# A state space layer: its two outputs summed in PSUM, and one step of its power table made a copy

## The chip, the cores and the metric

The kernel runs on one core of a Trainium2 chip. The metric is the device time of one launch in microseconds (us). A profiled execution of the same program gives, for every engine, when each instruction ran and what it waited for. The engines are TensorE (PE in the profile; its weight loads are PEld), VectorE (DVE), ScalarE (ACT), GpSimd (POOL) and SyncE (SP, which here only issues DMAs). Each engine works through its own queue in order.

## The reference

`x` is (1, 4096, 512). A cross attention layer with a state space part (`_L0_xattn_ref`) is added to it, and then a quantized feed-forward layer with a depthwise convolution (`_L0_ffn_ref`). The part that matters here is the state space layer `s4d`, which convolves each of the 512 channels with a kernel of its own, over all 4096 positions:

```python
def s4d(x, log_dt, A_re, A_im, C_re, C_im, D_skip):
    dt = jnp.exp(log_dt)
    A = A_re + 1j * A_im
    C = C_re + 1j * C_im
    dtA = dt[:, None] * A
    dC = C * (jnp.exp(dtA) - 1.0) / A
    powers = jnp.exp(dtA[:, :, None] * jnp.arange(L))
    K = 2.0 * jnp.einsum('dn,dnl->dl', dC, powers).real
    ...
    y = jnp.fft.irfft(xf * Kf.T[None], n=n, axis=1)[:, :L]   # y = causal convolution of x with K
    return y + x * D_skip
```

A channel has 64 complex states. `powers` holds the powers of exp(dt A) of each state.

## The kernel before

The program has three stages, one after the other: attention (until about 1675 us of the profile), `state_space` (about 1685 to 2222 us) and `feed_forwards` (the rest). The change touches `state_space` alone.

`state_space` cuts the 4096 positions into 32 chunks of 128, and the 512 channels into 8 groups of 64. A channel pair with its 2 x 64 states fills the 128 partitions, so a group is 32 pairs. For a group `g` the work is:

- `powers(g, k)` and `top(g, k)`, for each half `k` of the group (16 pairs): a tile `pt` of 128 x 16 x 2 (real, imaginary) x 128 that holds the powers 0 to 127 of each state. Column 0 is set to 1 + 0i once, by two memsets on POOL for each of the five tiles (L1093, L1094). Each level of a doubling multiplies the columns known so far by the power 2^lv and writes as many new ones: two multiplications into temporaries (L1130, L1131) and a sum into `pt` (L1132), all on DVE, 32 elements per partition at level 0, 64 at level 1, up to 1024 at level 5. The last level, `top`, shares its work between ACT (L1138, 16 instructions) and DVE (L1148, and the sum L1154 in `top_sum`).
- `turn` and `chunk`: transposes of `pt` on PE (L1168), copied out by ACT (L1171), and products with `x` on PE (L1180), copied by ACT (L1184) into `ht`, the state that each chunk adds.
- `scan_inside`, `scan_over`, `scan_into`: DVE turns these into the state at the start of each chunk (`times`, L1200 to L1202, with the sums L1214, L1219 and L1225).
- `outputs`: DVE multiplies the states with the output table (L1235 to L1237, in two halves of 16 chunks; L1239 puts the kernel's own row in front), and ACT copies the products `z` into `sz` (L1242).
- `between(g, u)`, u = 0 to 3: PE multiplies `sz` with `pt` into PSUM (L1255); ACT copies that into a tile `y` (`yg`) of 128 x 4 x 128 (L1261); POOL adds `D_skip` to column 0 (L1263). Partitions 32m of `y` hold the convolution's kernel (128 taps) of a channel; the others hold what earlier chunks give to this one. Eight DMAs for two tiles write the kernel rows to DRAM (`kd`).
- `load_k` reads `kd` back as a Toeplitz matrix `hk`, and `inside(g, u)` multiplies it with `x` on PE: 16 products of 32 rows x 128 columns into one PSUM tile `ps_h` (L1285), which has two buffers.
- `store(g, u)`: one DVE instruction (L1292) reads `ps_h`, adds `y` times `later`, and writes `y`; a DMA writes it to `yT`. `later` is a column of ones with zeros at partitions 0, 32, 64 and 96, so that the kernel rows are not added.

The order is written out by hand: the stage runs under a manual schedule for all five engines, so each engine has its instructions in program order. `round_(g)` for g from -2 to 8 mixes three groups: the scan and the outputs of `g`, the transposes and chunk products of `g + 1`, the powers of `g + 2`, and `inside` and `store` of `g - 1`. In a round, `store(g - 1, 0)` stands ahead of `scan_into(g)`, `store(g - 1, 1)` ahead of `outputs(g)`, and `store(g - 1, 2)` and `store(g - 1, 3)` behind `outputs(g)` and ahead of `turn(g + 1, 6)` and `powers(g + 2, 0)`. `inside(g - 1, u)` stands ahead of `turn(g + 1, u + 3)` and `chunk(g + 1, u + 2)`. Rounds 1 to 5 hold all of this. Rounds -2 to 0 have no `inside` and `store`, rounds 6 to 8 no `powers`, round 7 no `turn` and `chunk`, and round 8 only `inside` and `store` of the last group.

The temporaries of DVE (`temp`) come from one pool of five buffers of 128 x 1024, which are taken again as they come free. In `outputs`, ACT is the last reader of two of them (the two `z`).

Of the kernel before, what the change touches and what calls it, by code (L numbers as in the profile page):

```python
# [10 lines left out]
F32 = mybir.dt.float32  # L11
# [4 lines left out]
ALU = mybir.AluOpType  # L16
# [4 lines left out]
P = 128  # L21
# [853 lines left out]
LEVELS = 7  # L875
# [178 lines left out]
def state_space(env, io, tabs, x1r, yT):  # L1054
# [8 lines left out]
    tc, nc, ident = env.tc, env.nc, env.ident  # L1063
    with ExitStack() as ctx:
        def pool(name, bufs, **kw):
            return ctx.enter_context(tc.tile_pool(name=name, bufs=bufs, reuse_waits="tile", **kw))
# [11 lines left out]
        one = pool("s_one", 1)  # L1078
# [8 lines left out]
        tab, ptab, pts, tops, xg, ht, zs, bts, yg, hk, phs = ({} for _ in range(11))  # L1087
# [8 lines left out]
        def temp(n):  # L1096
            t = tmp.tile([P, 1024], F32, name="tmp")
            return t[:, :n]
# [18 lines left out]
        def powers(g, k):  # L1117
            q = slice(k * NSB, (k + 1) * NSB)
            pt = pts[g, k] = power_tiles[(2 * g + k) % len(power_tiles)]
            for lv in range(LEVELS - 1):  # L1120
                n = 2**lv
                sh = [P, NSB, 2, n]
                t1, t2 = (
                    temp(NSB * 2 * n).rearrange("p (q r n) -> p q r n", q=NSB, r=2)
                    for _ in range(2)
                )
                old = pt[:, :, :, :n]
                wr = ptab[g][:, 3 * lv, q].unsqueeze(2).unsqueeze(3).to_broadcast(sh)
                wi = ptab[g][:, 3 * lv + 1 : 3 * lv + 3, q].rearrange("p s q -> p q s")
                mul(t1, old, wr)  # L1130
                mul(t2, old, wi.unsqueeze(3).to_broadcast(sh))  # L1131
                add(pt[:, :, :, n : 2 * n], t1, t2[:, :, ::-1, :])  # L1132
# [147 lines left out]

        def inside(g, u):
            py = phs[g, u] = ps_h.tile([P, 4, P], F32, name="ps_h")
            for c in range(16):
                r = slice(32 * (c % 4), 32 * (c % 4) + 32)
                nc.tensor.matmul(  # L1285
                    py[r, c // 4, :], xg[g][:, :, 16 * u + c], hk[g, u, c // 8][:, c % 8, :],
                    start=True, stop=True,
                )

        def store(g, u):  # L1290
            y = yg.pop((g, u))
            nc.vector.scalar_tensor_tensor(y, y, later, phs.pop((g, u)), ALU.mult, ALU.add)  # L1292
            c0 = g * GC + 16 * u
            nc.sync.dma_start(
                bass.AP(yT.tensor, yT.offset + c0 * T, [[P, P], [4 * T, 4], [1, P]]), y
            )


        later = one.tile([P, 1], F32, name="later")
        dskip = one.tile([P, NPAIR // 2], F32, name="dskip")  # L1300
        sz = one.tile([P, 2, 2, NT, GP], F32, name="sz")
        load(0, 0, T_CHUNK)
        load(0, T_CHUNK, NTAB)
        nc.sync.dma_start(dskip, io["D_skip"])
        nc.gpsimd.memset(later, 1.0)
        for m in range(4):
            nc.gpsimd.memset(later[32 * m : 32 * m + 1, :], 0.0)

        def zeros():
            nc.gpsimd.memset(sz[:64, :, 1, :, :], 0.0)  # L1310
# [7 lines left out]
        def round_(g):  # L1318
# [16 lines left out]
            for u in range(4):  # L1335
                if back:
                    inside(g - 1, u)
                    if u < 2:
                        load_k(g - 1, u + 2)
                if n1 and u < 3:  # L1340
                    turn(g + 1, u + 3)
                    chunk(g + 1, u + 2)
                if back and u < 2:
                    store(g - 1, u)
                if u == 0 and now:
                    scan_into(g)
# [6 lines left out]
            if back:  # L1353
                store(g - 1, 2)
                store(g - 1, 3)
# [3 lines left out]
            if n2:  # L1359
                powers(g + 2, 0)  # L1360
                top(g + 2, 0)
# [14 lines left out]
            if n2:  # L1376
                powers(g + 2, 1)
                top_sum(g + 2, 0)
                top(g + 2, 1)
# [565 lines left out]
def block_kernel(tc, io, out):  # L1945
    with ExitStack() as ctx:
        env = Env(tc, ctx)
        env.n_tiles = NT
        dp = ctx.enter_context(tc.tile_pool(name="scratch", bufs=1, space=DRAM))
        x1r = dp.tile([T, D], F32, name="x1r")  # L1950
        film_out = dp.tile([T, 2 * D], F32, name="film_out")
        tabs = dp.tile([NTAB, P, NPAIR], F32, name="tabs")
        yT = dp.tile([D, T], F32, name="yT")
        x2 = dp.tile([T, D], F32, name="x2")
        xq = dp.tile([D, T], BF16, name="xq")
        dq = dp.tile([T], F32, name="dq")
        undo = env.c.tile([P, 2], F32, name="undo")

        def rest():
            state_space(env, io, tabs, x1r, yT)  # L1960
            feed_forwards(env, io, film_out, yT, x2, xq, dq, undo, out)

        bad = env.c.tile([P, 1], I32, name="bad")
        with tc.tile_pool(name="flags", bufs=1, reuse_waits="tile") as fp:
            missed = fp.tile([P, NT * H], F32, name="missed")
            masked = fp.tile([P, 1], F32, name="masked")
            env.nc.gpsimd.memset(masked, 0.0)
            attention(env, io, x1r, film_out, missed, masked, tabs)
            unlike(env, missed, masked, bad)
        rest()  # L1970
        n = env.nc.values_load(bad[0:1, 0:1], min_val=0, max_val=P * NT * H + G)
        with tc.If(n > 0):
            attention_general(env, io, x1r, film_out)
            rest()
# [71 lines left out]
```

## Time and profile before

| | |
|---|---|
| timed runs (us) | 3597.01, 3689.06, 3704.32; median 3689.06 |
| the profiled execution: its time | 3598.88 us |
| its span | 3597.1 us |
| busy in the span: PE, PEld, DVE, ACT, POOL | 3100.3, 1894.4, 3047.9, 1995.1, 976.4 us |
| granted TensorE clock over the span | 0.907 of full speed |
| `store` L1292, DVE, 128x512 | 32 instructions, mean 749 ns |
| copy of `y` L1261, ACT, 128x512 from PSUM | 32 instructions, mean 589 ns |
| levels 0 of `powers`, DVE, 128x32: L1130, L1131, L1132 | 16 of each, mean 200, 198 and 215 ns |

A row of the timeline has the start, the time that it lasts, the engine, the line, what is written from what, and a count where like instructions are merged; in brackets stands the idle time before it and what ended it. A matmul on float32 operands leaves two records, so `inside` with its 16 products shows x32. Consecutive DVE instructions overlap a little, so the time from one start to the next says better what an instruction costs than its own duration.

### The profile page before, as it was taken

The page shows a single profiled execution, that of the slowest core. Times are in us where ns is not written, and L with a number is a line of the kernel's source. Part 1 is how long each engine was busy: PE and PEld are TensorE (multiplying, and loading weights), DVE is VectorE, ACT ScalarE, POOL GpSimd, SP SyncE. Part 2 cuts the span into 40 slices and gives each one's busy share as a digit, 9 for nine tenths or more (in the row PEclk, how much of TensorE's full clock was granted, in tenths as well). Part 3 has the DMA queues.
Part 4 walks back from the last instruction along what each step waited for, and adds up shares of the span by engine and source line. Part 5 has one row for each costly group of instructions (what it writes and reads, how often), then busy time and mean ns, then how long its engine had stood idle before and what let it go on. Part 6 is the DMA issues. An engine that isn't in the chain of part 4 may idle for free. (4 is left out here: it accounts for less than half of the span.)

```text
span 3597.1 us, 48276 instructions
## 1 busy us (share of the span) xinstructions
PE 3100.3 (86%) x14970; PEld 1894.4 (53%) x15014; DVE 3047.9 (85%) x9455; ACT 1995.1 (55%) x3739; POOL 976.4 (27%) x1623
## 2 busy tenths in 40 slices
PE   7899999999999999994777774989998999999975
PEld 3444444444444444442776773656665666666642
DVE  5999999999999999988899984777777777777777
ACT  3777777777777777762655541124444444444445
POOL 2222232223333332221000001223433333334422
PEclk8899999999999999997777775999999999999987
DMA  7676766677666667664254437732223333232211
GB/s 197 128 135 136 142 132 132 134 144 140 136 136 136 131 131 145 132 134 118 47 126 103 125 80 239 216 95 55 55 63 57 63 62 68 55 69 55 52 33 47
DMA packets 355862, 394.19 MB, mean 110 GB/s; under 512 B 112741, under 2 KB 249959, under 8 KB 355210
## 3 DMA queue, kind: packets, MB, share of 16 engines
q0 software_dynamic: 51872, 161.82, 25.2%
q1 hardware_dynamic: 303722, 229.20, 25.0%
q8 instruction: 120, 1.97, 0.2%
q14 instruction: 148, 1.21, 0.1%
HBM read 171.31 MB, written 62.15 MB: 65 GB/s over the span
## 5 line engine op out<-in xcount | busy, mean ns | idle before, releaser
L597 DVE MAX8 cand<-s 128x8 f32<-128x89 f32 (+1 forms) x4608 | 715.3, 243 | 18.1 <-ACT s L584 18.1
L693 PE MATMUL po<-ctxn,aT 124*128 124x384 f32 (+1 forms) x1664 | 642.2, 531 | 14.4 <-ACT aT L681 14.3
L1533 PE MATMUL ph<-hT,w 128*128 128x256 f32 x2048 | 498.9, 388 | 0.5 <-ACT hT L1522 0.5
L1544 PE MATMUL po<-w,gt 128*128 128x512 f32 x1024 | 481.6, 592 | 0.0
L1690 ACT ACTIVATE cv<-pb,cb,cw 128x256 f32<-128x256 f32 (+1 forms) x272 | 149.8, 551 | 597.2 <-DVE pb L1687 591.3
L584 ACT ACTIVATE s<-ps 128x802 f32<-128x802 f32 (+1 forms) x512 | 400.2, 835 | 133.7 <-PE ps L580 133.6
L693 PEld LDWEIGHTS po<-ctxn,aT 124*128 124x128 f32 (+1 forms) x1664 | 327.5, 207 | 278.5 <-issue 75.6
L655 ACT ACTIVATE s<-s,lb 128x1601 f32<-128x1601 f32 x256 | 419.2, 1638 | 98.6 <-POOL lb L644 98.4
L619 DVE SCALAR_TENSOR_TENSOR s<-s,m 128x3202 f32<-128x3202 f32 x128 | 455.4, 3558 | 6.8
L1533 PEld LDWEIGHTS ph<-hT,w 128*128 128x128 f32 x2048 | 384.0, 195 | 61.2 <-issue 10.0
L718 PE MATMUL po<-wvf,acT 128*128 128x512 f32 x768 | 363.8, 610 | 0.6 <-ACT acT L708 0.6
L1699 DVE SCALAR_TENSOR_TENSOR cv<-pb,cw,cv 128x256 f32<-128x256 f32 (+1 forms) x544 | 252.6, 464 | 46.6 <-ACT cv L1690 36.9
L1678 PE MATMUL pb<-xw,w1q 128*128 128x258 bf16 (+1 forms) x1088 | 172.9, 285 | 123.5 <-DVE cv L1699 113.5
L659 POOL DMA_DIRECT2D s<-s x96 | 129.4, 1348 | 545.8 <-ACT s L655 180.4
L1768 POOL TENSOR_TENSOR cv<-cv,scb 128x512 f32<-128x512 f32 (+1 forms) x136 | 181.0, 1347 | 323.5 <-ACT scb L1763 323.5
L580 PE MATMUL ps<-kT,qT 32*128 32x401 f32 (+1 forms) x2048 | 259.9, 552 | 8.3 <-ACT s L584 8.3
L1687 DVE TENSOR_TENSOR pb<-pb,sx 128x258 f32<-128x258 f32 (+1 forms) x272 | 112.1, 412 | 182.1 <-PE pb L1678 180.5
L1544 PEld LDWEIGHTS po<-w,gt 128*128 128x128 f32 x1024 | 192.3, 190 | 134.3 <-issue 118.6
L1678 PEld LDWEIGHTS <-w1q 128*128 128x128 bf16 x1088 | 102.8, 103 | 290.9 <-DVE cv L1699 174.2
L718 PEld LDWEIGHTS po<-wvf,acT 128*128 128x128 f32 x768 | 135.3, 189 | 181.0 <-issue 164.0
L676 PE MATMUL pt<-ident,s 128*124 128x128 f32 x832 | 136.2, 293 | 105.3 <-DMA s<-s 84.9
L1538 ACT ACTIVATE gt<-ph,b 128x256 f32<-128x256 f32 x256 | 120.7, 472 | 184.3 <-PE ph L1533 184.1
(310 smaller groups left out, 5017.4 us busy)
## 6 DMA issues: line engine op xcount, KB each, us to landing
s<-s POOLq DMA_DIRECT2D x96, 1602.0 KB, 11.8
hk<-kd SPq DMA_DIRECT2D x64, 512.0 KB
film_out<-f SPq DMA_DIRECT2D x32, 512.0 KB
xt<-in_x SPq DMA_DIRECT2D x63, 256.0 KB
ft<-film_out SPq DMA_DIRECT2D x31, 512.0 KB
qT<-qd SPq DMA_DIRECT2D x128, 64.0 KB
xu<-in_x SPq DMA_DIRECT2D x32, 256.0 KB
x1r<-xr SPq DMA_DIRECT2D x32, 256.0 KB
```

Of the source, the lines that this page charges most:

```text
L580: nc.tensor.matmul(ps[:, j - j0, :n], qT[i][r, h, :], kT[r, h, c0 : c0 + n], start=True, stop=True,)
L584: nc.scalar.activation(sq[:, j0 : j0 + 2, c0 : c0 + n], ps[:, :, :n], AF.Copy, scale=QSCALE * TINY)
L597: nc.vector.max(out=cand[:, :, b], in_=s[:, b * CHW : min((b + 1) * CHW, G)])
L619: nc.vector.scalar_tensor_tensor(s[:, :G], s[:, :G], m8[:, KTOP - 1 : KTOP], s[:, :G], ALU.is_lt, ALU.subtract, accum_out=missed[:, k : k ...
L655: nc.scalar.activation(part, part, AF.Exp, bias=lbs[k][:, 1:2], scale=-1.0 / TINY)
L693: nc.tensor.matmul(pas[i][:, :DV], aTs[i][:w, c, :], ctxn[:w, c, :], start=(c == 0), stop=(c == NG - 1),)
L718: nc.tensor.matmul(po, acTs[i][:, c, :], wvf[:, c, q * D : (q + 1) * D], start=False, stop=(c == NDV - 1),)
L1533: nc.tensor.matmul(ph[:, :W], w1[:, d, c * P : (c + 1) * P], hTs[b][:, d, :], start=(d == 0), stop=(d == ND - 1),)
L1544: nc.tensor.matmul(pos[b * TB + k], gs[b, c][:, k * P : (k + 1) * P], w2[:, c, :], start=(c == 0), stop=(c == NH - 1),)
L1678: nc.tensor.matmul(ph[:, : n + 2], w1q[:, d, c * P : (c + 1) * P], bit["xw", j][:, d, : n + 2], start=(d == 0), stop=(d == ND - 1),)
L1699: nc.vector.scalar_tensor_tensor(cv, ph[:, tap : tap + n], cw[:, c, tap : tap + 1], cv, ALU.mult, ALU.add)
L1768: nc.gpsimd.tensor_mul(cv, cv, bit["scb", j][:, :n].unsqueeze(1).to_broadcast([P, 2, n]))
```

## The change

In `powers`, level 0 is taken out of the loop. Column 0 is 1 + 0i, so column 1 is the first power itself, and one DVE copy writes it from the table:

```diff
-            for lv in range(LEVELS - 1):
+            w = ptab[g][:, 0:2, q].rearrange("p s q -> p q s")
+            nc.vector.tensor_copy(pt[:, :, :, 1], w)
+            for lv in range(1, LEVELS - 1):
```

`later` becomes a 128 x 128 identity whose columns 0, 32, 64 and 96 are zero. In `inside`, PE first multiplies the whole tile `y` by it into `ps_h` (128 x 512, float32), and the 16 products add to that. In `store`, ACT copies the sum from PSUM to `y`:

```diff
         def inside(g, u):
             py = phs[g, u] = ps_h.tile([P, 4, P], F32, name="ps_h")
+            nc.tensor.matmul(
+                py.rearrange("p q l -> p (q l)"), later, yg[g, u].rearrange("p q l -> p (q l)"),
+                start=True, stop=False,
+            )
             for c in range(16):
                 r = slice(32 * (c % 4), 32 * (c % 4) + 32)
                 nc.tensor.matmul(
                     py[r, c // 4, :], xg[g][:, :, 16 * u + c], hk[g, u, c // 8][:, c % 8, :],
-                    start=True, stop=True,
+                    start=False, stop=(c >= 12),
                 )
 
         def store(g, u):
             y = yg.pop((g, u))
-            nc.vector.scalar_tensor_tensor(y, y, later, phs.pop((g, u)), ALU.mult, ALU.add)
+            nc.scalar.copy(y, phs.pop((g, u)))
...
-        later = one.tile([P, 1], F32, name="later")
+        later = one.tile([P, P], F32, name="later")
...
-        nc.gpsimd.memset(later, 1.0)
-        for m in range(4):
-            nc.gpsimd.memset(later[32 * m : 32 * m + 1, :], 0.0)
+        nc.gpsimd.tensor_copy(later, ident)
+        nc.gpsimd.memset(later.rearrange("p (m a) -> p m a", m=4)[:, :, 0], 0.0)
```

## The prediction

> **What bounds the kernel now.** I read the page's slices first, then the busy times of one stretch, then the groups by shape, then the timelines of DVE, ACT and PE over one round. The change lies in slices 19 to 25 (about 1685 to 2222 us), where DVE is fuller than PE and the TensorE clock is low:
>
> ```profile
> PE   7899999999999999994777774989998999999975
> DVE  5999999999999999988899984777777777777777
> PEclk8899999999999999997777775999999999999987
> 1860.00:1920.00 60.00, 45.92 (x448) 43.79 (x448) 57.78 (x104) 30.70 (x87) 2.32 (x5) 0.74 0.48 116
> ```
>
> The last line is one round (round 2 runs from 1860.30 to 1920.54, 60.24 us): PE 45.92 us busy, DVE 57.78, ACT 30.70, clock 0.74. DVE's row has no idle time with a releaser anywhere in it, so what is taken off DVE shortens the round until another engine is late. The groups and DVE's timeline give the prices:
>
> ```profile
> L1292 DVE SCALAR_TENSOR_TENSOR yg<-yg,later,ps_h 128x512 f32<-128x512 f32 x32 | 23.4, 749 | 34.6 <-PE ps_h L1285 34.3
> L1261 ACT COPY yg<-ps_y 128x512 f32<-128x512 f32 x32 | 18.2, 589 | 34.0 <-PE ps_y L1255 18.3 <-issue 14.2 <-DMA kd<-yg 1.4
> L1239 DVE COPY tmp<-tabb 128x64 f32<-128x64 f32 x8 | 1.6, 195 | 0.3
> ...
> 1876.44 0.75 DVE L1292 SCALAR_TENSOR_TENSOR yg<-yg,later,ps_h 128x512 f32<-128x512 f32 x1
> 1877.10 0.62 DVE L1200 TENSOR_TENSOR tmp<-ht,tabb 128x448 f32<-128x448 f32 x1
> ...
> 1895.49 0.20 DVE L1130 TENSOR_TENSOR tmp<-pt,taba 128x32 f32<-128x32 f32 x1
> ...
> 1896.15 0.23 DVE L1130 TENSOR_TENSOR tmp<-pt,taba 128x64 f32<-128x64 f32 x1
> ```
>
> From start to start a `store` costs DVE 0.66 us, and level 0 also 0.66. What can be late next is the chain over ACT and PE in the same round:
>
> ```profile
> 1887.69 0.84 ACT L1184 COPY ht<-ps_u 64x124 f32<-64x124 f32 x4 [1.07 <-PE ps_u L1180]
> 1890.76 2.10 ACT L1242 COPY sz<-tmp 64x1024 f32<-64x1024 f32 x2 [2.23 <-DVE tmp L1239]
> 1894.29 2.10 ACT L1242 COPY sz<-tmp 64x1024 f32<-64x1024 f32 x2 [1.42 <-DVE tmp L1237]
> ...
> 1874.20 2.01 PE L1285 MATMUL ps_h<-hk,xg 128*32 128x128 f32 x32
> 1879.56 1.29 PE L1285 MATMUL ps_h<-hk,xg 128*32 128x128 f32 x32
> 1896.44 6.33 PE L1255 MATMUL ps_y<-pt,sz 128*64 128x128 f32 x64 [4.79 <-ACT sz L1242]
> ...
> 2149.33 0.69 DVE L1200 TENSOR_TENSOR tmp<-ht,tabb 128x512 f32<-128x512 f32 x1 [11.09 <-ACT ht L1184]
> 2165.05 0.75 DVE L1292 SCALAR_TENSOR_TENSOR yg<-yg,later,ps_h 128x512 f32<-128x512 f32 x1 [2.08 <-PE ps_h L1285]
> ...
> 2302.54 1.73 PE po L1544 x4
> ```
>
> ACT waits only 1 to 2 us ahead of its `sz` copies, and PE's first `inside` of the round took 2.01 us where the later ones took 1.29. The last line, from the chain, is two 128x512 float32 products of the feed-forward stage (four records).
>
> **The change part by part.**
>
> *Level 0.* Three instructions (0.66 us) become one copy. The nearest row is L1239, 0.195 us; followed by an instruction that needs its result it takes 0.24 us, as L1132 at level 0 does (1907.40 to 1907.64). Gain 0.42 us a call. Of the 16 calls two (round -1) end in waits for ACT (3.92, 1.11 and 1.72 us before 1744.14) and gain nothing; 14 gain 5.9 us.
>
> *The store on DVE.* 20 instructions lie in rounds 1 to 5: 20 x 0.66 = 13.2 us. In round 6 two stand ahead of `outputs` (1.3 us), and the other two lie ahead of the 11.09 us wait and gain nothing. In round 7 two stand ahead of `outputs`, and the first waits 2.08 us for PE: 3.4 us, all of it ahead of the `sz` copies that PE waits for. The last store of round 8 becomes an ACT copy of 0.59 us (L1261, same shape, also from PSUM): nothing. Sum with level 0: 23.8 us.
>
> *The store on ACT.* Four copies of 0.54 to 0.59 us a round, 2.3 us. ACT is busy 30.7 of 60, and before `sz` it only fills waits. The pair behind `outputs` stands ahead of `turn(6)`'s copies: in rounds 1 to 5 PE is then in `between` (6.33 us), which hides it. In round 6 `turn` 6 and 7 and the chunks follow at once, and DVE waits for them (11.09 us): 1.1 us lost. SP's `yT` DMAs of that pair go out about 2 us later; behind them SP has the table and `x` loads of later groups, and `kd` writes that are not ready for another 10 us.
>
> *The product on PE.* Two records of 512 columns: warm 1.73 / 2 = 0.87 us. Cold, by `inside` (2.01 against 1.29) it is 1.35 us, by L1180 (3.52 against 1.96 in the same round) 1.55; I take L1180's ratio, as it has full-height weights too, and twice the warm price (1.73) as the far end. With 1.55 for the first of a round and 0.87 for three this is 4.2 us a round. `y` is ready a round earlier, so its data costs no wait. Behind it on PE stand `inside`, `turn`, `chunk`; for these waits ACT, whose `ht` copies of chunk 4 stand ahead of `sz`. Three products lie ahead of them (3.3 us): they end at 28.2 + 3.3 = 31.5 us of the round instead of 28.2. DVE will have the first `z` at 30.2 - 1.3 = 28.9. So ACT, not DVE, sets `sz`: its four copies (4.2 us) end at 35.7, against 36.1 today.
>
> *The wait that this adds.* ACT's `sz` copies are the last readers of two of DVE's five temporaries. `powers` comes to the second at its second to fourth level; today that is just after ACT is done (1896.39). With the stores and level 0 gone DVE gets there at about 34.3 us of the round and waits until 35.7, about 1.4 us. At the end of the round the chain through `top`, `between` and chunk 7 now ends 1.2 us ahead of DVE (1919.25 to 1920.54); it shortens with `powers` and stays 0.7 ahead. Bounds: no wait, if the buffers come free in another order; 2.6 us, which is all that the stores gain. I take 1.4 for rounds 1 to 5 (7 us) and 0.5 for round 0, which has no products: 7.5 us.
>
> *The ends.* Round 6: the products delay ACT's `sz` the same way, so its 1.3 us are lost too. Round 7: `inside` waits for `hk`; the products lie in these waits, except some 0.4 us. Round 8: the last two tiles are ready 0.7 to 1.4 us apart, and cold products stand between: 0.6 us lost (0 if warm, 1.0 at 1.73). `later`: POOL's memsets took 0.70 us from 1679.37; a copy of 128x128 lies between 0.18 (L75, one column) and 1.26 us (L1495, four times as wide), nearest perhaps 0.4, plus a memset of 0.12: nothing, within 0.7 either way.
>
> *The sum.* 23.8 - 7.5 - 1.1 - 1.3 - 0.4 - 0.6 = 12.9 us, 0.4%: about 3586 us on the profiled execution's 3598.88 (span 3597.1 and 1.8 around it). That execution lies at the lowest of the three timed runs; the median is 3689.06, 90 us above it, and nothing in this trace says where those 90 us go. I take the difference off the median: 3676 us. The low group, by the same sum 3584, may be the median next time and has to be in the range.
>
> [...] The low price of the product rests on the rows of L1544, where each record has a weight load of its own (190 ns) and still four records take 1.73 us, so the loads are hidden. [...]
>
> **The rivals.** (a) DVE stays the bound everywhere, with no wait at the temporaries: 23.8 less the 1.1 and 0.4 of rounds 6 and 7 is 22 us, 3577 on the profile, 3667 on the median. For it: five buffers, and PE idle 14 of 60 us. Against it: ACT's 1 to 2 us of slack. (b) The products slow DVE. DVE's 128x448 operations take 1.39 and 1.21 us instead of 0.62 at 1879.49 and 1883.19, when `inside` runs, and not when L1255 does. If the products do the same for 4.2 us a round, DVE loses about 2.2 us x 6 rounds = 13: no change, 3600 or 3690. (c) Slower: the chain over PE becomes the round. Every product at 1.73 us puts `sz` at 37.6 and the end of chunk 7 at 59.4 us of the round; DVE, held at the temporaries, ends at 60.2, where it ends now. So above 1.75 us a product the rounds get longer, by four times the excess: at 2.1 us 7 us in rounds 1 to 5, 4 in round 6 and 1.5 in round 8, less the 4 kept outside: 3608 or 3698. Over 2% (72 us) it would need more than 4 us a product, which no row supports. (d) The change does nothing for the end because the round is bound elsewhere already: against it stands DVE's row without a wait.
>
> **How the numbers follow.** My forecast (a gain of 6 to 18 us) has 0.5, (a) 0.2, (b) 0.15, (c) 0.1, (d) 0.05. All of these lie within 2%, which is about what a measurement of this kernel can tell from no change; the three runs themselves lie 3% apart. For that, and for what I have not seen, I leave 0.08 for faster and 0.05 for slower. The likeliest case alone gives 3671 to 3683 on the median. The range goes from the low group with a full gain (3575) to the highest run with no gain (3704), less a little: 3574 to 3700.
>
> **What would show it.** In the changed profile DVE should have no L1292, and its groups of 128x32 should be one copy near 0.2 us. ACT should have 32 copies of 0.59 us at the store. The product should take 0.87 us in most places. A wait of 1 to 2 us on ACT `sz` should stand at one of the first levels of `powers` once a round; rounds should last 58 to 59 us, against 60.24, and 57 without that wait. The forecast is wrong if DVE waits for `ht` at the start of a round, if DVE's rows are longer beside the product, or if the stage from 1685 to 2222 us is longer than now.

## The result, and the profile after

The changed kernel took 3573.26 us, the median of 7 runs (3569.68 to 3682.59), beside 3597.66 us for the kernel before, the median of 7 runs (3594.59 to 3704.32). The ratio is 0.9928, with a 95% interval of 0.9914 to 0.9943: 26 us or 0.7% less, which counts as no change at 2%. Runs of both kernels fall into two groups about 2.8% apart; the ratios compare the lower group alone, two of the three runs that the prediction started from lay in the upper one, and the state space stage is as long in a profile of the upper group (516.8 us) as in one of the lower (516.1).

The profile read here is that of a second run of the changed kernel (label after_again, span 3565.7 us against 3597.1 before). Its slices 19 to 25, round 2 (57.03 us; the columns are those of the line shown before), and groups of the state space stage by shape:

```profile
PE   7899999999999999995687876989989999999975
DVE  5999999999999999998999983777777777777776
PEclk8899999999999999997788787999999999999987
1848.85:1905.88 57.03, 44.55 (x456) 40.12 (x456) 54.87 (x97) 34.20 (x91) 2.87 (x5) 0.85 0.50 122
```

```profile
L1291 PE MATMUL ps_h<-hk,xg 128*32 128x128 f32 x1024 | 47.0, 322 | 16.4 <-DMA hk<-kd 16.4
L1285 PE MATMUL ps_h<-yg,later 128*128 128x512 f32 x64 | 40.9, 726 | 0.0
L1291 PEld LDWEIGHTS ps_h<-hk,xg 128*32 128x32 f32 x1024 | 36.9, 198 | 48.2 <-DMA hk<-kd 24.8 <-issue 23.4
L1298 ACT COPY yg<-ps_h 128x512 f32<-128x512 f32 x32 | 24.9, 801 | 33.6 <-PE ps_h L1291 24.3 <-DMA hk<-kd 8.9
L1203 DVE TENSOR_TENSOR tmp<-ht,tabb 128x448 f32<-128x448 f32 x32 | 24.7, 773 | 0.0
L1121 DVE COPY pt<-taba 128x32 f32<-128x32 f32 x15 | 2.9, 193 | 0.0
```

L1292 is gone from DVE, level 0 is one copy of 193 ns (L1121), and the store is an ACT copy (L1298), of 801 ns in the mean and not the 589 of L1261. DVE is busy 54.87 of 57.03 us where it was busy 57.78 of 60.00, so it is still the fullest engine. PE has the products in addition (L1285, two records each). In round 2 it is yet busy no longer, 44.55 us against 45.92, with the granted clock at 0.85 and not 0.74; over rounds 1 to 5 it is busy 46.2 us a round in the mean against 44.2, and the clock is 0.82 against 0.78.

Cut at the same instructions (the last one that makes the tables, L1050; level 1 of group 0; the start of each round on DVE; the first load of the next stage), the stage fell from 541.92 to 516.09 us:

| Part | before (us) | after (us) | gain | predicted gain |
|---|---|---|---|---|
| tables to level 1 of group 0 | 6.14 | 5.29 | 0.85 | 0.84 for both rows |
| from there to round 0 | 58.38 | 55.38 | 3.00 | |
| round 0 | 55.42 | 54.59 | 0.83 | 0.34 |
| rounds 1 to 5, the mean of one | 60.62 | 57.25 | 3.37 | 2.1 |
| round 6 | 46.65 | 46.22 | 0.43 | -1.1 |
| rounds 7 and 8, to the next stage's load | 72.21 | 68.34 | 3.87 | 2.4 |
| sum (rounds 1 to 5 count five times) | 541.92 | 516.09 | 25.8 | 12.9 |

The other 5.6 us of the span's 31.4 lie in attention and in the feed-forward stage, which the change does not touch. What there is to explain is a gain twice the predicted one, 6.5 us of it in rounds 1 to 5, where the wait that I had put at 1.4 us a round does not show.

### The profile page after: what moved, and what is told of

It reads as the page before. It is cut to its first block, busy times and chain, and to the rows that moved or that the text cites. A ratio compares the mean times of both kernels' runs of the same rounds, so it can differ in the third digit from the quotient of the medians.

```text
span 3668.6 us, 48302 instructions
## 1 busy us (share of the span) xinstructions
PE 3175.3 (87%) x15034; PEld 1918.4 (52%) x15078; DVE 3028.2 (83%) x9391; ACT 2017.1 (55%) x3771; POOL 1197.9 (33%) x1620
## 3 DMA queue, kind: packets, MB, share of 16 engines
q8 instruction: 120, 1.97, 0.2%
## 4 chain that ended last, share of the span: by engine, by line
PE 40%; DVE 31%; ACT 10%; POOL 7%; DMA 6%; issue 5%; SPq 0%; POOLq 0%; ACTq 0%; DVEq 0%
PE po L693 10%; PE ph L1538 8%; PE po L1549 7%; DVE cand L597 4%; DMA s<-s 4%; ACT s L584 3%; PE pp L1789 3%; PE ps L580 2%; DVE s L619 2%; PE pb L1683 2%; PE po L718 2%; ACT s L655 2%; DVE cv L1704 2%; DVE bn_st L69 2%; DVE cv L1722 2%
## 5 line engine op out<-in xcount | busy, mean ns | idle before, releaser
L693 PE MATMUL po<-ctxn,aT 124*128 124x384 f32 (+1 forms) x1664 | 653.7, 539 | 63.7 <-ACT aT L681 63.7
L580 PE MATMUL ps<-kT,qT 32*128 32x401 f32 (+1 forms) x2048 | 289.8, 582 | 79.8 <-ACT s L584 79.8
L580 PEld LDWEIGHTS ps<-kT,qT 32*128 32x128 f32 x2048 | 98.6, 192 | 201.5 <-ACT s L584 122.0
```

Of the source, the lines that this page charges most:

```text
L580: nc.tensor.matmul(ps[:, j - j0, :n], qT[i][r, h, :], kT[r, h, c0 : c0 + n], start=True, stop=True,)
L693: nc.tensor.matmul(pas[i][:, :DV], aTs[i][:w, c, :], ctxn[:w, c, :], start=(c == 0), stop=(c == NG - 1),)
```

## The experiments

The theory after the result: DVE stays the bound in every round, because it comes back to the buffer of the second `z` later than I had put it, after ACT has already let it go. The rivals: the product costs time that something else gives back; the wait is there in another shape; the gain belongs to the copy of level 0 and not to the store. "Stage" below is the table's sum, 541.92 before and 516.09 in the changed kernel.

**The changed kernel again** (after_again, no edit).

> The changed kernel once more, for a profile beside the others. Theory A (DVE is the bound of rounds 0 to 5, the product on PE and the copy on ACT are hidden, and no wait at the temporaries takes anything back): ratio 0.993, about 25 us off, with rounds of 57 us and under 0.5 us of waits for ACT at the levels of the powers. Rival B (the wait at the temporaries and the delay by the products take 8 us back, and something outside the rounds gives it instead): the same time, but rounds 1 to 5 longer than 58 us.

Measured: 0.9943 [0.9929, 0.9957] of the time before; the stage as in the table.

**One part at a time.** copy_alone has only the copy at level 0, psum_alone only the sum in PSUM:

```diff
# copy_alone, against the kernel before
-            for lv in range(LEVELS - 1):
+            w = ptab[g][:, 0:2, q].rearrange("p s q -> p q s")
+            nc.vector.tensor_copy(pt[:, :, :, 1], w)
+            for lv in range(1, LEVELS - 1):
# psum_alone, against the changed kernel
-            w = ptab[g][:, 0:2, q].rearrange("p s q -> p q s")
-            nc.vector.tensor_copy(pt[:, :, :, 1], w)
-            for lv in range(1, LEVELS - 1):
+            for lv in range(LEVELS - 1):
```

> Only the first doubling is a copy; the outputs are added on DVE as before. Theory A: 0.42 us for 14 calls and up to 1 us at the start of the stage, 6 to 8 us off (ratio 0.998). If the whole change gains more than its two parts, or less, they meet somewhere: rival B has the wait at the temporaries only with both, so the parts alone would gain more than the whole.

> Only the product on PE and the copy on ACT; level 0 stays three DVE instructions. Theory A: 20 stores of 0.66 us in rounds 1 to 5, 3.4 us in round 7, nothing in rounds 6 and 8: 16 to 18 us off (ratio 0.995). Rival B: 7 us are lost in waits at the temporaries or behind the products, 9 to 11 us off (0.997).

Measured: copy_alone 0.9978 [0.9968, 0.9988], 7.9 us less, and its stage is 8.1 us shorter; psum_alone 0.9961 [0.9947, 0.9974], 14.0 us less, its stage 17.4 us shorter. The stages add up, 8.1 + 17.4 = 25.5 against 25.8 for both, so neither part lives off the other. Of the copy's 8.1 us, 3.0 lie between level 1 and round 0 (55.34 us, as in the changed kernel; psum_alone has 58.49, where the kernel before has 58.38); rounds 0 to 5 gain what was costed, 0.8 us each in the mean, and rounds 6 to 8 lose 0.8 together.

**Without the product** (no_product: the product is left out, so `y` lacks what earlier chunks give).

```diff
-            nc.tensor.matmul(
-                py.rearrange("p q l -> p (q l)"), later, yg[g, u].rearrange("p q l -> p (q l)"),
-                start=True, stop=False,
-            )
...
-                    start=False, stop=(c >= 12),
+                    start=True, stop=True,
```

> The changed kernel without the product on PE: what earlier chunks give to the output is left out. Theory A: the product is hidden in rounds 1 to 5 and costs at most 1 to 3 us in rounds 6 and 8: within 3 us of the changed kernel. Rival B: the products delay ACT's sz copies and DVE behind them by 1 us a round and more: 6 to 10 us faster than the changed kernel.

Measured: 0.9940 [0.9921, 0.9959]; rounds 1 to 5 last 57.06 us in the mean, against 57.25 with the product, and the stage 516.8 us. The product costs nothing where it stands.

**Two and four products.** Each product starts the PSUM tile anew, so the sum holds `y` once.

```diff
-            nc.tensor.matmul(
+            for rep in range(2):    # four_products: range(4)
+                nc.tensor.matmul(
```

> The changed kernel with the product on PE issued twice for each tile (the second overwrites the first, so the result is the same): about 1 us more of PE per tile, 4 us a round. Theory A: PE and ACT have some 3 us of room before PE's wait for sz becomes DVE's: rounds 1 to 5 grow by 0 to 1 us each, rounds 6 and 8 by 3 to 5 us together; 3 to 10 us slower than the changed kernel. Rival B: the products are on the path already, 3 to 4 us a round, 20 to 25 us slower.

> The product issued four times for each tile (the last counts): about 3 us more of PE per tile, 12 us a round, of which 9 lie ahead of the sz copies. Theory A: past the room of some 3 us each round grows by what is left, 5 to 7 us; with rounds 6 to 8 about 40 to 50 us slower than the changed kernel. Rival B: 9 to 12 us a round from the start, 60 to 70 us slower.

Measured: two_products 0.9953 [0.9939, 0.9967], stage 525.7 us, 9.6 more than with one; by the ratios it is only 3.6 us slower than after_again, and their intervals overlap. The four runs of four_products took 3603.89, 3608.16, 3703.51 and 3710.26 us; its stage takes 556.3 us, and rounds 1 to 5 last 63.26 us, 6.0 more than with one product. DVE now waits for ACT's `sz` copies early in `powers`, though not for the buffer that I had named. DVE's timeline in the kernels with two and with four products, one wait of each, and beside the first ACT's four `sz` copies:

```profile
1941.04 0.29 DVE L1132 TENSOR_TENSOR tmp<-pt,taba 128x128 f32<-128x128 f32 x1 [1.01 <-ACT sz L1244]
```

```profile
1938.41 4.73 ACT L1244 COPY sz<-tmp 64x1024 f32<-64x1024 f32 x4
```

```profile
1959.34 0.43 DVE L1133 TENSOR_TENSOR tmp<-pt,taba 128x256 f32<-128x256 f32 x1 [6.66 <-ACT sz L1244]
```

ACT copies the two `z` one after the other, with two copies for each. The wait until 1941.04 ends as the second of the four copies does, so it is for the first `z`; ACT is through with the second only 2.1 us later. In each of rounds 1 to 5 the waits of both kernels end in this way. So the chain through PE and ACT has room for the first product (about 4 us a round); the second costs 1.1 us a round and the third and fourth 4.9 together. Rival (c) of the prediction had the right place: PE's chain does become the round, but only once there is more than one product.

**The wait, forced.** The changed kernel has five temporaries. four_temps has four; z_at_level_1 keeps five and makes level 1 write into the last `z` itself.

```diff
# four_temps
-        tmp = pool("s_tmp", 5)
+        tmp = pool("s_tmp", 4)
# z_at_level_1
+                if lv == 1 and k == 0 and last_z:
+                    t1 = last_z[0][:, : NSB * 2 * n].rearrange("p (q r n) -> p q r n", q=NSB, r=2)
...
-                z, t = (
-                    temp(NT * GP).rearrange("p (a r q) -> p a r q", r=2, q=GP) for _ in range(2)
-                )
+                zf, tf = temp(NT * GP), temp(NT * GP)
+                last_z[:] = [zf]
+                z, t = (f.rearrange("p (a r q) -> p a r q", r=2, q=GP) for f in (zf, tf))
```

> The changed kernel with four temporaries of DVE instead of five, so that the powers come to a buffer that ACT still reads at level 2 and not at level 5. Theory A: the wait that was predicted now appears, 1 to 1.5 us in each of rounds 0 to 5 at level 2 of the powers, 4 to 8 us slower than the changed kernel. Rival: there is slack behind it and rounds stay at 57 us.

> The changed kernel, but the first temporary of level 1 of the powers is the buffer of the second z, which ACT still reads there (the wait that was predicted, forced at the earliest level). In the changed kernel DVE begins level 1 at about 33.1 us of a round and ACT ends with sz at 35.6, and it meets that buffer only at level 5, at 38.2. Theory A: 2 to 3 us of wait in rounds 0 to 5 and 12 to 16 us more than the changed kernel, so the predicted wait had a real price and only its place was wrong. Rival C: the time comes back behind it, where another engine is late anyway, and rounds 1 to 5 stay within 1 us of 57.3.

Measured: four_temps 0.9941 [0.9927, 0.9955], rounds 1 to 5 of 56.58 to 57.54 us, one wait of 0.44 us. My expectation fell, and its premise with it: the trace lists with an instruction the semaphores that it waits for and those that it updates, and in this kernel the instructions of `powers` that wait for one that ACT updates stand at levels 1 and 4, not at 2. So the buffer of the second `z` comes back 1.1 to 1.4 us after ACT is done with it, and the run does not force the wait. z_at_level_1 takes 0.9974 [0.9960, 0.9989]; its rounds 1 to 5 last 59.56 us in the mean, and by the ratios it is 11 to 17 us slower than the changed kernel. DVE's waits for ACT in the stretch from 1680 to 2220 us (total, times, longest) and one of them in the timeline:

```profile
DVE tmp L1135 <- ACT sz L1247: 13.7, 6, 2.8
```

```profile
1827.48 0.24 DVE L1135 TENSOR_TENSOR tmp<-pt,taba 128x64 f32<-128x64 f32 x1 [2.05 <-ACT sz L1247]
```

Six waits of 2.05 to 2.82 us, one in each of rounds 0 to 5, and rounds 2.3 us longer. The wait that I predicted is real when the buffer is needed at level 1. It is longer than my 1.4 us, in part because level 1 starts 0.72 us ahead of level 2. In the changed kernel the buffer is simply not needed there.

**The store on DVE.** dve_copy lets DVE do the copy out of PSUM.

```diff
-            nc.scalar.copy(y, phs.pop((g, u)))
+            nc.vector.tensor_copy(y, phs.pop((g, u)))
```

> The changed kernel with the copy out of PSUM on DVE instead of ACT: the product on PE stays. Theory A: DVE has back 20 instructions of about 0.65 us in rounds 1 to 5 and the wait for PE in round 7, so all that the store brought is gone and only the first doubling's 6 to 8 us stay: ratio to before 0.997 to 0.998. If part of the gain came from the product itself (PE kept busy and its clock up), more than 8 us stay.

Measured: 0.9989 [0.9978, 1.0000], stage 536.2 us, 5.7 less than before and 20.1 more than the changed kernel. The copy takes DVE 0.71 us in the mean where the old instruction took 0.75, and the 5.7 us that are left are less than the copy of level 0 gives alone (8.1). What the store gains comes from its leaving DVE, not from being a copy; the sum in PSUM by itself gives DVE next to nothing.

**The old level 0 in the first group.** old_level_0_first_group has the copy only from group 1 on.

```diff
-            for lv in range(1, LEVELS - 1):
+            if g:
+                w = ptab[g][:, 0:2, q].rearrange("p s q -> p q s")
+                nc.vector.tensor_copy(pt[:, :, :, 1], w)
+            for lv in range(1 if g else 0, LEVELS - 1):
```

> The changed kernel, but for the first group alone level 0 is the three old instructions. It tells whether the 3.0 us that every kernel with the copy gained between the first level 1 and round 0 hang on when PE starts (its clock came up 12.1 us after its first transpose with the copy, 17.3 us without). Theory A: 0.66 us come back ahead of level 1 and PE's first transposes are 0.4 us later; if the clock goes by when PE starts, it comes up 17 us after them again and round 0 starts 58.4 us after level 1; if it goes by anything else in the kernel, 55.8.

Measured: 0.9954 [0.9940, 0.9968], stage 519.5 us, and from level 1 to round 0 58.46 us, about as in the kernel before (58.38). So the 3.0 us hang on the first group's copy. PE's timeline there, the changed kernel first and then this one:

```profile
1702.16 1.97 PE L1170 MATMUL ps_t<-ident,pt 128*128 128x128 f32 x8 [26.73 <-DVE pt L1156]
...
1713.14 2.13 PE L1182 MATMUL ps_u<-xg,bt 128*128 128x64 f32 x16
1715.09 1.05 PE L1170 MATMUL ps_t<-ident,pt 128*128 128x128 f32 x8
```

```profile
1705.76 1.97 PE L1171 MATMUL ps_t<-ident,pt 128*128 128x128 f32 x8 [27.82 <-DVE pt L1157]
...
1716.75 3.52 PE L1183 MATMUL ps_u<-xg,bt 128*128 128x64 f32 x16
1720.07 1.90 PE L1171 MATMUL ps_t<-ident,pt 128*128 128x128 f32 x8
...
1724.11 1.05 PE L1171 MATMUL ps_t<-ident,pt 128*128 128x128 f32 x8
```

Eight transposes take 1.97 or 1.90 us at first and 1.05 later. The first fast ones stand 12.9 us behind the first of all in the changed kernel and 18.4 us in the other, with the same order of work between. The traces also record the granted clock. In those of the kernel before and of the changed kernel it is either 0.5 or 1 of full speed, and the points at which it changes (160 stretches of one value before, 152 after) lie 3.413 us or a multiple of it apart within a trace. Counted from the start of the last instruction that makes the tables (L1050), PE's first transposes come after 26.0 us with the copy in the first group and after 27.0 to 27.1 without. The full clock comes after 37.3 to 37.8 us with it, in all eleven traces of such kernels (37.4 in the one of the changed kernel's first run), and after 44.2 to 44.3 us in the three traces without it (44.2 in the kernel before). So where PE's first transposes came about 1.1 us earlier, the full clock came 6.8 us earlier, twice 3.413. What brings the full clock, these runs do not show.

**The weights of `inside`.** Beside `inside`, DVE and ACT are slow: L1203 takes 773 ns in the mean and L1298 801. `inside` loads 32 channels' worth of `x` as weights, and its 32 elements of a partition stand 256 bytes apart. contiguous_weights loads 32 neighbouring elements instead (other values of `x`, so the convolution within a chunk is not the reference's). x_by_channel keeps the values and moves them: ACT copies `x` of a group once into a tile `xc` with the channels first, ahead of `top` two rounds before `inside` uses it, and one buffer each of `xg`, the temporaries and `yg` makes room.

```diff
# contiguous_weights
-                    py[r, c // 4, :], xg[g][:, :, 16 * u + c], hk[g, u, c // 8][:, c % 8, :],
+                    py[r, c // 4, :], xg[g][:, c, :NT], hk[g, u, c // 8][:, c % 8, :],
# x_by_channel
+        def by_channel(g):
+            xc[g] = xgp.tile([P, GC, NT], F32, name="xc")
+            nc.scalar.copy(xc[g], xg[g].rearrange("p a c -> p c a"))
...
-                    py[r, c // 4, :], xg[g][:, :, 16 * u + c], hk[g, u, c // 8][:, c % 8, :],
+                    py[r, c // 4, :], xc[g][:, 16 * u + c, :], hk[g, u, c // 8][:, c % 8, :],
```

> The changed kernel with other weights in the 16 products of inside: 32 neighbouring elements of a row of x instead of 32 elements 256 bytes apart, so the output is not that of the reference. DVE and ACT instructions that run beside these products take up to twice as long (1.45 us instead of 0.62 for 128x448, 1.2 instead of 0.59 for the copy of ps_h). If the stride of the weight loads does that, the rows return to 0.62 and 0.59 and rounds 1 to 5 get 2 us shorter; if the four column tiles that read hk at once do it, nothing changes.

> The changed kernel, and ACT copies each group's x to a tile in which the 32 chunks of a channel are neighbours, so that the weight loads of inside read 128 neighbouring bytes a partition; the copy stands in front of top, where ACT waits 3.8 us for DVE. (For space x has two buffers instead of three, the temporaries and y four instead of five.) If the stride of the weight loads is what slows DVE and ACT: rounds 1 to 5 of about 54.6 us, as with the contiguous weights, less 2 us lost in round -1, where ACT is late; 13 to 16 us faster than the changed kernel, ratio to before 0.990. If it was the values of those other weights and not their place: rounds stay at 57.3 us or get longer by the copy.

Measured: contiguous_weights 0.9886 [0.9870, 0.9901], rounds 2 to 5 of 54.6 us. x_by_channel 0.9896 [0.9881, 0.9912], 3557.26 us in the median of 5 runs, 37 us less than the kernel before; by the ratios that is 12 to 17 us below the changed kernel's two measurements. Groups of x_by_channel by shape:

```profile
L1119 ACT COPY xc<-xg 128x2048 f32<-128x2048 f32 x8 | 31.5, 3938 | 0.1
L1295 PEld LDWEIGHTS ps_h<-hk,xc 128*32 128x32 f32 x1024 | 29.0, 121 | 50.6 <-DMA hk<-kd 28.0 <-issue 21.9
L1207 DVE TENSOR_TENSOR tmp<-ht,tabb 128x448 f32<-128x448 f32 x32 | 19.8, 618 | 0.0
L1302 ACT COPY yg<-ps_h 128x512 f32<-128x512 f32 x32 | 18.1, 588 | 32.4 <-PE ps_h L1295 17.2 <-DMA hk<-kd 11.8 <-issue 3.0
```

The weight load falls from 198 to 121 ns, the DVE group from 773 to 618 and the ACT copy from 801 to 588, though `inside` still runs beside them. Within the changed kernel the rows part the same way: the 12 ACT copies that run beside these loads take 0.96 to 1.37 us, the 20 that do not 585 to 599 ns, and all 24 of DVE's 128 operations of 128x448 from round 0 on that take over 0.66 us lie beside them. In x_by_channel the copies beside the loads take 585 to 589 ns. Rounds 2 to 5 last 54.46 to 54.69 us. In round -1 the new copy costs 3.6 us (58.98 us from level 1 to round 0), and in round 1 DVE waits 2.36 us for `sz`.

## Why the prediction was right and wrong, point by point

**Class: right. Size: low by half.** "Within 2%" came out (0.9928). The time, 3573.26 us, lies 0.7 us below the range's low end of 3574. Even the sum without any wait or loss, 23.8 us, ends at 3575; the stage gained 25.8, because the start gave 3.0 us more than was in the sum.

**The level.** Taking the difference off the median of three runs put the level 90 us too high. On the profiled execution's own level the forecast was 3586 us; the measured difference of 26 us off 3598.88 would be 3573. The level was not something that the trace could say; the size was.

**Level 0 and the store on DVE: right.** Two copies and four stores were to give 4 x 0.66 + 2 x 0.42 = 3.48 us of DVE's time a round. Rounds 1 to 5 gave 3.37, and round 0, with two copies alone, 0.83 of 0.84.

**The product: right in place, slightly low in price.** From its start to the next instruction's start it takes 1.94 us at the first product of rounds 1, 4 and 5 and 0.97 to 0.99 at all others of rounds 1 to 6, against 1.55 and 0.87. PE's timeline of the changed kernel in round 4 (from 1963.00 us on DVE):

```profile
1976.93 2.00 PE L1285 MATMUL ps_h<-yg,later 128*128 128x512 f32 x2
1978.87 1.57 PE L1291 MATMUL ps_h<-hk,xg 128*32 128x128 f32 x32
...
1983.05 1.06 PE L1285 MATMUL ps_h<-yg,later 128*128 128x512 f32 x2
1984.04 1.25 PE L1291 MATMUL ps_h<-hk,xg 128*32 128x128 f32 x32
```

It delays ACT's `ht` copies of chunk 4 by 3.5 us (they end at 30.0 us of the round in the mean, against 26.5 in no_product), where I had 3.3. In four_products four of them in a row take 3.54 to 3.56 us in most places, so each one beyond the first adds 0.86 us, where 0.87 was costed from L1544. That price holds the product's weight loads, two to a product in the changed kernel's profile (L1285, 64 of 222 ns in the mean).

**"The wait that this adds": the step that failed.** I wrote that `powers` comes to the second of the two `z` buffers "at its second to fourth level" and waits there until 35.7 us, 1.4 us in each of rounds 1 to 5. ACT's time was right: `sz` ends at 35.6 us of the round in the mean. So was DVE's at level 2, 33.8 to 34.3 us. What DVE takes there is another buffer. The changed kernel's round 4 again, ACT first and then DVE:

```profile
1992.96 0.84 ACT L1186 COPY ht<-ps_u 64x124 f32<-64x124 f32 x4 [1.08 <-PE ps_u L1182]
1993.82 4.86 ACT L1244 COPY sz<-tmp 64x1024 f32<-64x1024 f32 x4
1998.70 1.08 ACT L1298 COPY yg<-ps_h 128x512 f32<-128x512 f32 x2
```

```profile
1996.31 0.20 DVE L1121 COPY pt<-taba 128x32 f32<-128x32 f32 x1
1996.54 0.23 DVE L1132 TENSOR_TENSOR tmp<-pt,taba 128x64 f32<-128x64 f32 x1
...
2001.49 1.22 DVE L1132 TENSOR_TENSOR tmp<-pt,taba 128x1024 f32<-128x1024 f32 x1
```

ACT is done with the second `z` at 1998.68. The instructions of `powers` whose semaphores wait for ACT stand at levels 2 and 5 in rounds 0 to 5, and I take them to be the ones that come back to the two `z`: with more products the waits at the first of them end with the first `z`. So the second `z` comes back at level 5, which starts at 2001.49, 2.8 us after ACT is done. The first `z`, which comes back at level 2, is read earlier; there DVE waits now and then, 0.38 and 0.45 us in this profile, in rounds 1 and 5, and in no other round. z_at_level_1 shows the wait for the second `z` when it is forced.

In the kernel before, these instructions stand at levels 1 and 3 in rounds 1 to 5, so "second to fourth level" was true of that kernel. Level 3 of its round 2:

```profile
1897.73 0.42 DVE L1130 TENSOR_TENSOR tmp<-pt,taba 128x256 f32<-128x256 f32 x1
```

I carried this over to the changed kernel, with DVE there at 34.3 us, which is level 2. But the edit itself moves the buffer: in rounds 1 to 5 of copy_alone the second `z` comes back at level 3, in dve_copy at level 4, in psum_alone and in the changed kernel at level 5. Even at level 3 the wait in the changed kernel would have been some 0.8 us a round and not 1.4 (an estimate: level 3 would start 0.85 us after level 2, and ACT's ends are those of the trace). Why the built program gives the buffers out in another order, the runs do not show. In rounds 1 to 5 this step was 6.5 us of the error, in round 0 0.5.

**The ends: mis-sized, by 3.0 us together.** In round 6 I had 1.1 us lost, and 0.43 was gained; in rounds 7 and 8 I had 2.4 gained, and 3.87 were. The sum had 1.3 us of delay by the products in round 6 and 1.0 us in rounds 7 and 8. They did not come: no_product, which has none, takes 46.28 us for round 6 and 69.68 for rounds 7 and 8, no less than the changed kernel. That is 2.3 of the 3.0 us; what the other 0.7 are, no run tells apart.

**The start: mis-sized, by 3.0 us.** The copy of the first group was costed on DVE alone, 0.84 us for its two calls, and 3.85 came. It also brought PE's first transposes 1.1 us earlier and PE's full clock in round -1 6.8 us earlier, a term that the sum did not have.

**The store on ACT: mis-sized, with little effect.** I had 0.54 to 0.59 us a copy; the mean is 801 ns, since 12 of the 32 run beside `inside`. Rounds 1 to 5 hardly show it: psum_alone shortens each by 2.46 us, where 2.64 was costed for DVE's four stores.

**The rivals.** (a), no wait at the temporaries, put the profile at 3577 us and came closest: DVE does stay the bound. (b), the product slows DVE, is not so: rounds without it are as long. The slow DVE rows beside `inside` that I took as its ground go with the weights of `inside`, which the change does not touch: of DVE's 128 operations of 128x448, 18 took over 0.66 us in the kernel before, and none in contiguous_weights. (c) begins beyond one product, at about 4 us a round. (d) fell: psum_alone and copy_alone both shorten the rounds.

## What to carry to other kernels

Before a wait for a shared buffer goes into a sum, follow that buffer through the pool to the instruction that writes it next, and do so in the changed program: here the edit that was to bring the wait moved the buffer from level 3 to level 5. When work moves from the full engine to others, ask how much room the chain over them has, and measure it by doubling the moved piece: here one product was free, two were nearly so, four were not. Where an engine's rows have two durations for one shape, look at what runs beside them: here that was worth another 12 to 17 us, which the change had not touched.

## What the runs showed of the hardware that was not expected

The weight loads of `inside`, which read 32 float32 elements 256 bytes apart, take 198 ns in the changed kernel, and 119 in contiguous_weights, where the elements are neighbours. DVE and ACT operations that run beside the strided loads take longer as well: a 128x448 operation of DVE as much as 1.55 us instead of 0.62, the 128x512 copy of ACT 801 ns in the mean instead of 588. The same groups in contiguous_weights:

```profile
L1291 PEld LDWEIGHTS ps_h<-hk,xg 128*32 128x32 f32 x1024 | 28.6, 119 | 49.2 <-DMA hk<-kd 26.8 <-issue 22.0
L1298 ACT COPY yg<-ps_h 128x512 f32<-128x512 f32 x32 | 18.1, 588 | 34.0 <-PE ps_h L1291 19.5 <-DMA hk<-kd 14.1
L1203 DVE TENSOR_TENSOR tmp<-ht,tabb 128x448 f32<-128x448 f32 x32 | 19.8, 618 | 0.0
```

With neighbouring elements a round is 2.6 us shorter. Why ACT and DVE take longer here, the runs do not show; that it goes with the stride of the weights, they do: in x_by_channel, with the values of `x` kept and only their places changed, the loads take 121 ns, the DVE group 618 and the ACT copy 588.
